# Longer runs in a transposed load, single buffers for small stores, and a new division of side work around a selective scan

## The chip, the cores and the metric

The kernel runs on one core of a Trainium2 chip. The metric is the device time of one execution in microseconds. A core has a matrix engine (TensorE, PE in the profile), VectorE (DVE), ScalarE (ACT), GpSimd (POOL) and SyncE (SP, which here issues all DMAs but the gathers), each with an instruction queue of its own that is worked off in order. 16 DMA engines serve the core.

## The reference, cut to what matters

Four layers over a tensor of 4 images, 128 channels and 128 x 128 pixels, each of the form x = x + f(group_norm(x)): a deformable 3x3 convolution (layer 0), a dilated convolution factored into three matrices (layer 1), a block around a two-dimensional selective scan (layer 2), and a 3x3 convolution that also takes differences of the channel sum (layer 3). The change concerns layer 2:

```python
x_flat = x.reshape(Bb, C, L)
x_t = x.transpose(0, 1, 3, 2).reshape(Bb, C, L)
x_hwwh = jnp.stack([x_flat, x_t], axis=1)
xs = jnp.concatenate([x_hwwh, jnp.flip(x_hwwh, axis=-1)], 1)
...
def step(h, inp):
    u, d, b, c = inp
    dA = jnp.exp(d[..., None] * A)
    h = h * dA + (d * u)[..., None] * b[:, :, None, :]
    y = jnp.einsum('bkcn,bkn->bkc', h, c)
    return (h, y)
...
return out_y[:, 0] + inv_y[:, 0] + wh_y + invwh_y
```

So the same image is scanned in four directions, two along rows and two along columns, with 16 states for each of 128 channels; the sums of the column directions come out in column order, and have to be read back in row order. Ahead of the scan lie a channel normalisation, projections and a depthwise convolution (layer2_pre); after it a normalisation, a gate, a projection and a second normalisation (layer2_post).

## The kernel before, in words

**Tiles.** An image is a matrix of 128 channels (partitions) by 16384 pixels, cut into 32 blocks of 512 pixels (four rows). Everything is float32. Between stages an image lives in DRAM.

**The scan.** `scan` (from L760) goes through 128 pairs of a direction and a block for each image, in the order of directions 0, 1, 3, 2. For each pair t it has four groups g of 32 channels, spread over 128 partitions as 32 channels x 4, and in each group four chunks: 16 chunks, each with one scan instruction on VectorE (L946) over 512 pixels. One such chunk is called a slot: 2048 slots an image, 8192 in all. For a group, a large VectorE product (L912) makes the inputs h from dub and bb; ScalarE makes the decays pa (L851, `decay`, into two PSUM buffers) and copies dub (L837, `inputs_up`); GpSimd multiplies the scanned h by cb (L885, `outputs`); TensorE sums over states (L862, `sums`) into yacc; `finish` copies yacc to y (L872) and stores it in yrow or ycol.

`prepare(t + 2)` (from L781) runs a piece at a time, one after each slot of t: a matmul pdt (L790), ScalarE's Abs into e (L795) and Relu into the first half of the tile steps (L798), more ScalarE work, a small matmul and its copy bc (L812), and four GpSimd instructions, the last of which (L822) writes the second half of steps. Steps and bc are then stored to DRAM (stepsd, bcd), and loaded back spread over the partitions (`spread_steps`, L830, two groups ahead; `spread_states`, L843).

At the start of an image nothing is running ahead, so two blocks are prepared at once:

```python
for t in range(2):
    for _ in prepare(t):
        pass
    fetch(t + 2)
flush()
```

**Stores.** `store` (L134) doesn't issue a DMA, it puts it on a list; `tick`, called once a slot, issues what is three ticks old, and `flush` issues all. All of it goes through SP's queue (L145, L149), as do all loads (L126), in the order of the program. An SP instruction that waits for its data or for a free buffer holds up those behind it.

**Side work.** While the scan of image b runs, the slots carry pieces of the other stages: layer2_post and layer3 of image b-1, then layer0_table, layer0, layer1 and layer2_pre of image b+1. `chain` gives each stage a weight; `together` advances the side work after each slot until its weighted progress has caught up with the scan's. A stage's weight thus decides over how many slots it is stretched. Weights: `head` (L1203) has layer0_table 12, layer0 28, layer1 14, layer2_pre 36; `tail` (L1206) has layer2_post 16, layer3 22; the rest of layer2_pre for image 0 has 18 (L1213). During the last scan the weights of `tail` are multiplied by 2.5, and layer2_post of the last image follows with 33 (L1217); it can take a block only once the last direction has summed it. The last image's layer3 runs alone at the end. Within a stage `weave` issues the steps of different blocks interleaved in a fixed order.

**Column sums.** In `layer2_post` (from L961), `fetch` (L987) loads for every CH = 16 image rows one tile ycols of 128 x 128 x 16 values from ycol (L992): its innermost run is 16 values, 64 bytes, at a distance of 512 bytes. `centre` multiplies four rows of it with a matrix (L1014), reading every 16th value. The transposed store of ucol in `layer2_pre` (cols, L744) works with CH = 32.

Of the kernel before, what the change touches and what calls it, by code (L numbers as in the profile page):

```python
# [10 lines left out]
F32 = mybir.dt.float32  # L11
# [99 lines left out]
def conv_preact_kernel(ctx: ExitStack, tc: tile.TileContext, a: dict, nb: int):  # L111
# [5 lines left out]
    dram = ctx.enter_context(tc.tile_pool(name="dram", bufs=2, space=DRAM))  # L117
    hp = ctx.enter_context(tc.tile_pool(name="sch", bufs=4))
    bp = ctx.enter_context(tc.tile_pool(name="scb", bufs=2))
    sp = ctx.enter_context(tc.tile_pool(name="scp", bufs=2))  # L120
    pss = ctx.enter_context(tc.tile_pool(name="scps", bufs=1, space=PSUM))
    psb = ctx.enter_context(tc.tile_pool(name="bgps", bufs=1, space=PSUM))

    def load(pool, src, shape, name, **kw):
        t = pool.tile(shape, F32, name=name, **kw)
        nc.sync.dma_start(t, src)  # L126
        return t
# [49 lines left out]

    xdt = load(const, a["xdt"], [DTR, NDIR, P], "xdt_sb")
    dtt = load(const, a["dtt"], [DTR, NDIR, P], "dtt_sb")
    wd = const.tile([P, NDIR, P], F32, name="wd")  # L180
    for k in range(NDIR):
        pw = bank(0, "pwd")
        nc.tensor.matmul(pw[:, 0:P], xdt[:, k, :], dtt[:, k, :], start=True, stop=True)
        nc.scalar.copy(wd[:, k, :], pw[:, 0:P])
    neg_a = load(const, a["alog"], [P, NDIR, NST], "neg_a")
# [5 lines left out]
    def blk(t, i):  # L191
        return t[:, i * N : (i + 1) * N]
# [567 lines left out]
    def scan(st, pull):  # L760
# [20 lines left out]
        def prepare(t):  # L781
# [13 lines left out]
            nc.scalar.activation(e, pdt, AF.Abs, bias=dtb)  # L795
            steps = sp.tile([P, 2, N], F32, name="steps")
            delta, du = steps[:, 0, :], steps[:, 1, :]
# [12 lines left out]
            nc.scalar.activation(one_e, one_e, AF.Identity, bias=minus)  # L810
            bc = sp.tile([2 * NST, N], F32, name="bc")
            nc.scalar.copy(bc, px[0 : 2 * NST])  # L812
# [56 lines left out]
        def finish(t):  # L869
            k, i, back, second = seq[t]  # L870
            y = sp.tile([P, N], F32, name="y")
            nc.scalar.copy(y, blocks[t]["y"])  # L872
            store(blk(ys[k % 2], i), y, of=ys)
            blocks[t] = None
            st["summed"] = t + 1 - 3 * NBLK
# [13 lines left out]
        for t in range(2):  # L889
            for _ in prepare(t):  # L890
                pass
            fetch(t + 2)
        flush()
# [7 lines left out]
        for t, (k, i, back, second) in enumerate(seq):  # L901
# [5 lines left out]
            for g in range(NG):  # L907
# [17 lines left out]
                if g == 3 and second:  # L925
                    c["before"] = load(sp, blk(ys[k % 2], i), [P, N], "before")
                for ng in range(NG):
# [33 lines left out]
    def layer2_post(st):  # L961
        CH = 16
        keep, stats_out = image("x3d"), new_stats(st["b"], 3)
        yrow, ycol = st["y"]
        urow = st["u"][0]
        with ExitStack() as s:
# [34 lines left out]
            def fetch_gate(i):  # L1001
                got["z", i] = load(lp, blk(st["z"], i), [P, N], "zl", bufs=5)
                got["y", i] = load(lp, blk(st["y1"], i), [HALF, N], "yl", bufs=5)

            def fetch_skip(i):
                got["x", i] = load(lp, blk(st["x2"], i), [P, N], "xl", bufs=4)

# [195 lines left out]
    def head(b):  # L1203
        return [(layer0_table(sts[b]), 12), (layer0(sts[b]), 28), (layer1(sts[b]), 14), (layer2_pre(sts[b]), 36)]

    def tail(b):  # L1206
        return [(layer2_post(sts[b]), 16), (layer3(sts[b]), 22)]

# [3 lines left out]
    for b in range(nb):  # L1212
        side = [(begun, 18)] if b == 0 else tail(b - 1)  # L1213
        if b < last:
            side += head(b + 1)
        else:
            side = [(stage, 2.5 * w) for stage, w in side] + [(layer2_post(sts[b]), 33)]  # L1217
        together(lambda pull: scan(sts[b], pull), chain(side))
# [85 lines left out]
```

## Time and profile before

| What | Time |
|---|---|
| Median of 3 runs | 23136.59 us (23130.67 to 23153.46) |
| The profiled execution itself | 23137.48 us |
| Its span, first to last instruction | 23135.7 us |
| VectorE busy | 18414.2 us (80%) |
| TensorE busy | 17549.8 us (76%) |
| GpSimd busy | 17326.7 us (75%) |
| ScalarE busy | 16509.2 us (71%) |
| DMA queue of SP, share of 16 engines' time | 50.2% |
| First scan instruction / last scan instruction | 2116.0 / 22807.9 us |

A line of the page's costliest groups names the line, the engine, the operation, what it writes and reads and its shape, how often it ran, then its busy time, the mean of one in ns, and the engine's idle time ahead of it with what ended most of that. TensorE works through a float32 matmul in two passes, so the records of matmuls are twice the number of matmuls in the code. TensorE's busy time is modelled and overlaps.

### The profile page before, as it was taken

What the parts mean: (1) busy time and instruction counts of PE and PEld (TensorE: products, weight loads), DVE (VectorE), ACT (ScalarE), POOL (GpSimd) and SP (SyncE); (2) the same over time, 40 slices, a digit from 0 to 9 for tenths busy, and PEclk for the clock granted to TensorE, in tenths of its full rate; (3) what the DMA queues carried; (4) which work ended last, traced back from release to release, by engine and by line L of the source; (5) the groups of instructions that cost most, each with busy time, mean ns of one, the idle gap of its engine ahead of it and who ended that gap; (6) DMA issues with size and microseconds to landing.
All of it is one profiled execution on the core that took longest, in us unless ns stands there. A gap on an engine that the chain in (4) does not pass through costs nothing. (4 is left out here: it accounts for less than half of the span.)

```text
span 23135.7 us, 180009 instructions
## 1 busy us (share of the span) xinstructions
PE 17549.8 (76%) x39144; PEld 6857.8 (30%) x39144; DVE 18414.2 (80%) x19279; ACT 16509.2 (71%) x37410; POOL 17326.7 (75%) x11422
## 2 busy tenths in 40 slices
PE   4558866667899897666789889666688978777778
PEld 1222322223333333222333334222233323233223
DVE  3553888888988799777897789877788789999973
ACT  5885768887677666788768676688877767666563
POOL 4762678888777877788876687788877678877773
PEclk7669987778999998777899999778799989899999
DMA  8775687777665958677766675877775667555664
GB/s 242 229 220 157 198 278 228 229 229 233 220 200 196 230 201 275 222 226 233 236 221 200 197 226 208 276 226 231 230 250 197 199 197 219 185 193 200 196 199 121
DMA packets 2557777, 5005.38 MB, mean 216 GB/s; under 512 B 1056832, under 2 KB 1328648, under 8 KB 2414352
## 3 DMA queue, kind: packets, MB, share of 16 engines
q1 hardware_dynamic: 2188048, 3785.60, 50.2%
q0 software_dynamic: 368640, 1208.25, 17.5%
q8 instruction: 317, 5.19, 0.1%
q14 instruction: 772, 6.32, 0.1%
HBM read 4065.12 MB, written 857.74 MB: 213 GB/s over the span
## 5 line engine op out<-in xcount | busy, mean ns | idle before, releaser
L885 POOL TENSOR_TENSOR h<-h,cb 128x1024 f32<-128x1024 f32 x4096 | 9620.6, 2357 | 3407.5 <-ACT carry L884 3261.6
L946 DVE TENSOR_TENSOR_SCAN h<-pa,carry,h 128x512 f32<-128x512 f32 x8192 | 10068.6, 1269 | 1601.4 <-ACT pa L851 1392.1
L862 PE MATMUL yacc<-h,gather_sb 128*128 128x512 f32 x16384 | 8716.5, 667 | 1293.3 <-POOL h L885 888.7
L851 ACT ACTIVATE pa<-spread,neg_a 128x512 f32<-128x512 f32 x8192 | 5616.0, 686 | 3173.9 <-DVE h L946 3143.2
L415 POOL DMA_INDIRECT g<-table,idx x4608 | 4391.2, 953 | 1543.8 <-issue 1116.2
L862 PEld LDWEIGHTS yacc<-h,gather_sb 128*128 128x128 f32 x16384 | 3331.8, 214 | 5889.4 <-issue 3897.2
L912 DVE TENSOR_TENSOR h<-dub,bb 128x2048 f32<-128x2048 f32 x2048 | 4641.1, 2266 | 430.6 <-ACT dub L837 421.7
L429 ACT ACTIVATE g<-g,wt 128x128 f32<-128x128 f32 x9216 | 2960.2, 391 | 1025.5 <-DMA g<-table,idx 1020.4
L452 PE MATMUL pst<-ident,v 128*128 128x128 f32 x4608 | 1193.7, 371 | 2475.2 <-DVE v L444 2232.2
L441 DVE TENSOR_TENSOR pw<-pw,g 128x512 f32<-128x512 f32 x2304 | 1604.3, 696 | 1641.9 <-ACT pw L429 1555.1
L452 PEld LDWEIGHTS pst<-ident,v 128*128 128x128 f32 x4608 | 727.5, 160 | 3892.8 <-issue 1628.1
L429 ACT ACTIVATE pw<-g,wt 128x128 f32<-128x128 f32 x4608 | 1690.9, 367 | 196.2 <-DVE v L444 84.2
L462 PE MATMUL acc<-smp,w_sb 128*128 128x512 f32 x2304 | 1610.2, 789 | 14.3 <-DVE x L469 11.3
L444 DVE SCALAR_TENSOR_TENSOR v<-g,wt,pw 128x128 f32<-128x128 f32 x4608 | 1292.8, 342 | 114.4 <-DVE pw L441 4.1
L837 ACT COPY dub<-spread 128x512 f32<-128x512 f32 x2048 | 1169.0, 571 | 131.0 <-DMA spread<-stepsd 131.0
L790 PE MATMUL pdt<-u,wd 128*128 128x512 f32 x1024 | 658.0, 729 | 795.2 <-DVE h L912 687.9
L884 ACT COPY carry<-h 128x2 f32<-128x2 f32 x4096 | 766.7, 187 | 677.9 <-DVE h L946 676.9
L806 PE MATMUL pxbc<-u,xbc_sb 128*128 128x512 f32 x1024 | 657.8, 728 | 655.0 <-DVE h L912 642.1
L1146 PE MATMUL p<-xn,w_l_sb 128*128 128x508 f32 (+2 forms) x2304 | 1102.0, 598 | 1.8 <-ACT xn L1125 1.8
L702 PE MATMUL px<-win,convw_sb 128*128 128x508 f32 (+1 forms) x1536 | 841.9, 630 | 6.8 <-DMA win<-win 6.8
L704 PE MATMUL py<-win,diag 128*64 128x508 f32 (+1 forms) x1536 | 836.1, 626 | 0.0
L816 POOL TENSOR_TENSOR e<-e,one_e 128x512 f32<-128x512 f32 x512 | 652.4, 1274 | 90.8 <-ACT one_e L810 90.8
(167 smaller groups left out, 16127.7 us busy)
## 6 DMA issues: line engine op xcount, KB each, us to landing
spread<-stepsd SPq DMA_DIRECT2D x2048, 512.0 KB
bb<-bcd SPq DMA_DIRECT2D x512, 1024.0 KB
cb<-bcd SPq DMA_DIRECT2D x512, 1024.0 KB
stepsd<-steps SPq DMA_DIRECT2D x512, 512.0 KB
table<-gt SPq DMA_DIRECT2D x512, 256.0 KB
g<-table,idx POOLq DMA_INDIRECT x4608, 3.8
u<-urow SPq DMA_DIRECT2D x256, 256.0 KB
yrow<-y SPq DMA_DIRECT2D x256, 256.0 KB
```

The costliest lines, as they stand in the source:

```text
L415: nc.gpsimd.indirect_dma_start(out=g[:, r].rearrange("p q c -> p (q c)"), out_offset=None, in_=table, in_offset=bass.IndirectOffsetOnAxis( ...
L429: nc.scalar.activation(pw[:, r * P : (r + 1) * P] if c == 0 else g[:, r, c, :], g[:, r, c, :], AF.Copy, scale=wv[:, r, q, k, c : c + 1],)
L441: nc.vector.tensor_add(pw, pw, g[:, :, c, :])
L444: nc.vector.scalar_tensor_tensor(v[:, r, :], g[:, r, 3, :], wv[:, r, q, k, 3:4], pw[:, r, :], ALU.mult, ALU.add)
L452: nc.tensor.transpose(pst[:, r * P : (r + 1) * P], v[:, r, :], ident)
L462: nc.tensor.matmul(got["a", i], w0[:, k, :], got.pop(("c", n)), start=k == 0, stop=k == KK - 1)
L837: nc.scalar.copy(p, blocks[t]["p", g][:, 1, :])
L851: nc.scalar.activation(pa, blocks[t]["p", g][:, 0, :], AF.Exp, scale=neg_a[:, k, n : n + 1])
L862: nc.tensor.matmul(c["y"], gather[:, g, :], c["h", g][:, ng, :], start=g == 0 and ng == 0, stop=last and not second,)
L885: nc.gpsimd.tensor_mul(h[:, sl, :], h[:, sl, :], cb[:, sl, :])
L912: nc.vector.tensor_tensor(h, c["pdu", g].unsqueeze(1).to_broadcast([P, NG, N]), c["bb"], ALU.mult)
L946: nc.vector.tensor_tensor_scan(o, f, o, carry[:, n : n + 1], ALU.mult, ALU.add)
```

## The change

Five things are done.

- Column sums are loaded for CH = 32 image rows at a time: tiles of 2 MB instead of 1 MB, with innermost runs of 128 bytes, half as many.
- Room for them: steps, bc, y and before get one buffer instead of two; zl and yl four instead of five; xl three instead of four.
- At the start of an image, `flush` is called after each prepared block, since with one buffer the first block's steps must be issued for storing before the second's are written.
- xdt and dtt, used once at the start, are put into a pool that is given back; the scan's pools are opened after that.
- Weights: layer0_table 11, layer0 27, layer1 13, layer2_pre 33, layer2_post 20, layer3 24; during the last scan those of `tail` are multiplied by 2.2.

```diff
@@ -175,13 +172,17 @@
-    xdt = load(const, a["xdt"], [DTR, NDIR, P], "xdt_sb")
-    dtt = load(const, a["dtt"], [DTR, NDIR, P], "dtt_sb")
     wd = const.tile([P, NDIR, P], F32, name="wd")
...
+    with tc.tile_pool(name="steps", bufs=1) as wp:
+        xdt = load(wp, a["xdt"], [DTR, NDIR, P], "xdt_sb")
+        dtt = load(wp, a["dtt"], [DTR, NDIR, P], "dtt_sb")
...
+    hp = ctx.enter_context(tc.tile_pool(name="sch", bufs=4))
+    bp = ctx.enter_context(tc.tile_pool(name="scb", bufs=2))
+    sp = ctx.enter_context(tc.tile_pool(name="scp", bufs=2))
@@ -793,7 +794,7 @@
-            steps = sp.tile([P, 2, N], F32, name="steps")
+            steps = sp.tile([P, 2, N], F32, name="steps", bufs=1)
@@ -808,7 +809,7 @@
-            bc = sp.tile([2 * NST, N], F32, name="bc")
+            bc = sp.tile([2 * NST, N], F32, name="bc", bufs=1)
@@ -868,7 +869,7 @@
-            y = sp.tile([P, N], F32, name="y")
+            y = sp.tile([P, N], F32, name="y", bufs=1)
@@ -889,6 +890,7 @@
         for t in range(2):
             for _ in prepare(t):
                 pass
+            flush()
             fetch(t + 2)
         flush()
@@ -923,7 +925,7 @@
-                    c["before"] = load(sp, blk(ys[k % 2], i), [P, N], "before")
+                    c["before"] = load(sp, blk(ys[k % 2], i), [P, N], "before", bufs=1)
@@ -959,7 +961,7 @@
     def layer2_post(st):
-        CH = 16
+        CH = 32
@@ -999,11 +1001,11 @@
-                got["z", i] = load(lp, blk(st["z"], i), [P, N], "zl", bufs=5)
-                got["y", i] = load(lp, blk(st["y1"], i), [HALF, N], "yl", bufs=5)
+                got["z", i] = load(lp, blk(st["z"], i), [P, N], "zl", bufs=4)
+                got["y", i] = load(lp, blk(st["y1"], i), [HALF, N], "yl", bufs=4)
...
-                got["x", i] = load(lp, blk(st["x2"], i), [P, N], "xl", bufs=4)
+                got["x", i] = load(lp, blk(st["x2"], i), [P, N], "xl", bufs=3)
@@ -1201,10 +1203,10 @@
-        return [(layer0_table(sts[b]), 12), (layer0(sts[b]), 28), (layer1(sts[b]), 14), (layer2_pre(sts[b]), 36)]
+        return [(layer0_table(sts[b]), 11), (layer0(sts[b]), 27), (layer1(sts[b]), 13), (layer2_pre(sts[b]), 33)]
...
-        return [(layer2_post(sts[b]), 16), (layer3(sts[b]), 22)]
+        return [(layer2_post(sts[b]), 20), (layer3(sts[b]), 24)]
@@ -1214,7 +1216,7 @@
-            side = [(stage, 2.5 * w) for stage, w in side] + [(layer2_post(sts[b]), 33)]
+            side = [(stage, 2.2 * w) for stage, w in side] + [(layer2_post(sts[b]), 33)]
```

More of the change, by code (lines that the diff above doesn't have):

```diff
@@ L117, in conv_preact_kernel @@
     dram = ctx.enter_context(tc.tile_pool(name="dram", bufs=2, space=DRAM))
-    hp = ctx.enter_context(tc.tile_pool(name="sch", bufs=4))
-    bp = ctx.enter_context(tc.tile_pool(name="scb", bufs=2))
-    sp = ctx.enter_context(tc.tile_pool(name="scp", bufs=2))
     pss = ctx.enter_context(tc.tile_pool(name="scps", bufs=1, space=PSUM))
@@ L175, in conv_preact_kernel @@
     nc.vector.memset(zero, 0.0)
-    xdt = load(const, a["xdt"], [DTR, NDIR, P], "xdt_sb")
-    dtt = load(const, a["dtt"], [DTR, NDIR, P], "dtt_sb")
     wd = const.tile([P, NDIR, P], F32, name="wd")
[L181 to L184, printed above, removed]
+    with tc.tile_pool(name="steps", bufs=1) as wp:
+        xdt = load(wp, a["xdt"], [DTR, NDIR, P], "xdt_sb")
+        dtt = load(wp, a["dtt"], [DTR, NDIR, P], "dtt_sb")
+        for k in range(NDIR):
+            pw = bank(0, "pwd")
+            nc.tensor.matmul(pw[:, 0:P], xdt[:, k, :], dtt[:, k, :], start=True, stop=True)
+            nc.scalar.copy(wd[:, k, :], pw[:, 0:P])
+    hp = ctx.enter_context(tc.tile_pool(name="sch", bufs=4))
+    bp = ctx.enter_context(tc.tile_pool(name="scb", bufs=2))
+    sp = ctx.enter_context(tc.tile_pool(name="scp", bufs=2))
     neg_a = load(const, a["alog"], [P, NDIR, NST], "neg_a")
```

## The prediction

> **What bounds the kernel now.** First the page's costliest groups, to see what one unit of the scan costs each engine. One slot is one scan instruction (L946); there are 8192, 2048 for each of four batches, and side work is dealt out between them.
>
> ```profile
> L885 POOL TENSOR_TENSOR h<-h,cb 128x1024 f32<-128x1024 f32 x4096 | 9620.6, 2357 | 3407.5 <-ACT carry L884 3261.6
> L946 DVE TENSOR_TENSOR_SCAN h<-pa,carry,h 128x512 f32<-128x512 f32 x8192 | 10068.6, 1269 | 1601.4 <-ACT pa L851 1392.1
> L912 DVE TENSOR_TENSOR h<-dub,bb 128x2048 f32<-128x2048 f32 x2048 | 4641.1, 2266 | 430.6 <-ACT dub L837 421.7
> ```
>
> A slot costs VectorE 1.269 + 2.266/4 = 1.836 us, whatever runs beside it. Since all 2048 slots of a batch are paid anyway, I count for each side stage its **excess**: its time minus 1.836 per slot. I then cut the trace at the first slot of each stage (the program's order gives the slots) and asked for busy time in each stretch. The columns are: length, busy PE, PE weight load, DVE, ACT, POOL, clock, DMA share, GB/s. Lines 1 to 5 are batch 0 (end of layer2_pre, then table, layer0, layer1, layer2_pre of the next batch); 6 to 11 are batch 1 (layer2_post, layer3, table, layer0, layer1, layer2_pre; batch 2 repeats it within 1%, layer2_post 592.8); 12 to 14 are batch 3 (layer2_post, layer3, its own layer2_post).
>
> ```profile
> 2115.90:2879.30 763.40, 687.26 (x1430) 237.59 (x1430) 619.27 (x439) 601.43 (x1102) 541.89 (x284) 0.97 0.59 192
> 2879.30:3337.80 458.50, 311.25 (x712) 125.82 (x712) 417.37 (x324) 286.72 (x574) 330.77 (x168) 0.85 0.89 301
> 3337.80:5570.40 2232.60, 1444.78 (x3459) 585.02 (x3458) 1808.67 (x2712) 1819.01 (x4944) 1887.35 (x1549) 0.79 0.70 227
> 5570.40:6115.70 545.30, 466.79 (x1011) 191.22 (x1010) 511.11 (x413) 354.26 (x697) 389.06 (x197) 0.94 0.73 242
> 6115.70:7585.00 1469.30, 1258.59 (x2592) 446.79 (x2592) 1207.92 (x857) 1084.39 (x2026) 1053.58 (x550) 0.95 0.58 195
> 7585.00:8188.80 603.80, 538.64 (x1091) 206.43 (x1092) 479.01 (x366) 440.41 (x867) 536.29 (x320) 0.96 0.89 233
> 8188.80:8868.80 680.00, 631.13 (x1513) 277.32 (x1512) 651.06 (x484) 422.48 (x844) 526.80 (x267) 0.97 0.58 204
> 8868.80:9277.60 408.80, 286.01 (x638) 117.50 (x637) 355.42 (x275) 248.09 (x493) 281.44 (x144) 0.80 0.90 302
> 9277.60:11386.30 2108.70, 1327.27 (x3283) 540.50 (x3283) 1671.41 (x2612) 1731.51 (x4755) 1763.93 (x1487) 0.78 0.71 227
> 11386.30:11853.50 467.20, 416.24 (x925) 173.43 (x925) 441.13 (x366) 307.69 (x605) 334.28 (x171) 0.96 0.78 255
> 11853.50:13156.60 1303.10, 1139.53 (x2338) 401.33 (x2338) 1019.11 (x722) 971.30 (x1790) 892.89 (x468) 0.94 0.58 192
> 18717.20:19999.00 1281.80, 1010.51 (x1955) 385.61 (x1956) 1152.33 (x848) 864.38 (x1731) 1101.68 (x608) 0.91 0.70 209
> 19999.00:21642.30 1643.30, 1279.62 (x2753) 517.88 (x2752) 1570.21 (x1138) 995.12 (x2013) 1300.08 (x660) 0.95 0.55 194
> 21642.30:22809.20 1166.90, 899.08 (x1688) 340.27 (x1688) 946.30 (x684) 713.64 (x1416) 899.70 (x492) 0.90 0.67 195
> ```
>
> The slots in these stretches are 350, 225, 525, 266, 682; 257, 358, 190, 443, 225, 575; 641, 880, 527. To see: layer3 runs on the VectorE floor (680.0 - 358 x 1.836 = 23 excess; 28 with 880 slots). layer2_post with 257 slots has 132 excess and POOL at 89%; with 641 it has 105. layer0 has 1295.
>
> Then the column sums and the matmul that reads them.
>
> ```profile
> L1014 PE MATMUL pd<-ycols,cmat_sb x256: 1017/1033/1043, 7610.5 to 22834.3; 128*128 128x512 f32 x128
> L992 SPq DMA_DIRECT2D ycols<-ycol x32: 547/594/685, 7575.6 to 22712.7; - x32
> ```
> ```profile
> L744 ACT COPY cols<-u x64: 1912/1957/2012, 1942.6 to 18661.9; 128x1024 f32<-128x1024 f32 x64
> ```
>
> Last, the start of a batch, in order of time (start, length).
>
> ```profile
> 7558.16 0.68 ACT L798 ACTIVATE steps<-pdt,vec_sb 128x512 f32<-128x512 f32 x1
> 7558.96 1.27 POOL L822 TENSOR_TENSOR steps<-steps,u 128x512 f32<-128x512 f32 x1
> 7568.69 0.79 SPq L149 DMA_DIRECT2D stepsd<-steps  x1
> 7571.83 2.59 SPq L830 DMA_DIRECT2D spread<-stepsd  x3
> 7578.30 16.32 SPq L126 DMA_DIRECT2D yrl<-yrow  x1
> ```
>
> The issue of yrl, just behind a ycols load, holds SP for 16.32 us.
>
> **What the skill says.** The Trainium skill, "DMA: Bandwidth & Descriptors", section on why small descriptors are slow: each packet carries a fixed cost beside its bytes. The trace agrees: by the semaphores, 1 MB of ycols in 64-byte runs lands a median of 17.6 us after issue, and 2 MB of ucol, stored in 128-byte runs, after 16.2; both have 16384 runs. The same page, on queues and rings: a ring is drained in order, so what is issued behind ycols waits; the 16.32 us above agrees. "SBUF — State Buffer", specifications: 16-byte lines, each crossing pays. L1014, stepping 64 bytes, takes 1033/512 = 2.02 ns an element where its neighbour L1012 takes 592/512 = 1.16; ScalarE stepping 128 bytes (L744) pays 1957/1024 = 1.91. So I take 128 bytes to cost what 64 do.
>
> **The change, part by part.** Compute instructions are unchanged in number; SP issues 16 fewer (9051 to 9035).
>
> *Shares.* The program's order after gives batches 1 and 2 layer2_post 320 slots, layer3 391, table 174, layer0 427, layer1 209, layer2_pre 527. Slopes of excess from the pairs above: table (45.4 - 60.0)/35 = -0.42 a slot, layer0 (1268.7 - 1295.4)/82 = -0.33, layer1 about 0, layer2_pre (217.1 - 247.4)/107 = -0.28. Donors therefore lose: table 16 x 0.42 = 7, taken as 9 since its DMA share is 0.90; layer0 16 x 0.33 = 5; layer2_pre 48 x 0.28 = 14; together +28. layer3 gains nothing. layer2_post: POOL's scan part is 526.8/358 = 1.47 a slot, so its own work is 536.3 - 257 x 1.47 = 158; with 320 slots POOL has 628. At today's 89% that is 706 us, at 93% (its share in the middle of the stage) 675; I take 690, fewer loads counted in. Excess 690 - 587.5 = 102, against 132: -30. Per batch -2; two batches -4.
> Batch 0: layer2_pre 370 first slots -6, table 218 +3, layer0 537 -4, layer2_pre 662 +6: -1. Batch 3: 54 slots pass from layer3 and the last stage to layer2_post (695, 833, 520); at 1.84 to 1.87 either way: 0. The last stage waits for the scan's blocks, so its share decides nothing.
>
> *Longer runs.* Eight ycols loads a batch become four, each about 17 us (bounds 16 to 20). VectorE's idle time around one in batch 3 exceeds that ahead of it by 2 us in the first stage and at most 5 in the last, where stretches with and without differ by 1.6. I take 2 and 1.5: 4 x 2 + 4 x 1.5 = -14. In batches 1 and 2 it is inside the 690. L1014 is taken at 0; the upper bound, twice its time, is 64 x 1.03 = 66 us of PE a stage.
>
> *Single buffers.* Relu into steps (L798) now waits until the last block's store has landed; behind it ScalarE queues dub and pa, and VectorE waits on those. For each block I compared landing and next Relu: the median slack is 8.8 us. Outside batch starts and two landings spoilt by a lost semaphore record, some 20 of 512 are late, 36 us together; pa is two deep, so half passes: +18 (0 to 36). bc has 16 us or more of slack, y 14, before 3: 0. At a batch start the second Relu ran at 7558.16; now it waits for du (7560.23) and its store (about 3 us): 5.2 later. SP has then already issued the first pair of stores, so the first spread goes about 3.5 us later, and nothing hides it: 4 x 3.5 = +14. (The added flush only orders those stores.)
> zl and yl with one buffer less would have waited in SP's queue on L1043 some 30 us per short stage, xl 12 on L1069; behind them stand spreads issued eight slots (about 18 us) early, which hides most: +6 (0 to 40).
> The hp, bp, sp pools opened later move addresses only: 0.
>
> **Sum** against the profiled execution (23137.5, span 23135.7): -1 - 4 - 14 + 18 + 14 + 6 = +19, so 23156; the median of the runs lies 1 us lower: 23155.
>
> **Rivals.** *Donors at their floors (slower).* In layer2_pre a returned slot saves only PE's scan share, (1258.6 - 1139.5)/107 = 1.11, so 48 slots cost 35 instead of 14; table by DMA 11, layer0 by ACT (1819.0 - 1731.5)/82 = 1.07, 12; layer1 10. That is 68 instead of 28, twice +40, and +9 in batch 0: 23244. For: PE 87 to 90% busy in layer2_pre, DMA 0.90 in table. Against: PE's time is modelled and overlaps, and the slopes above are measured. It decides from about 42 us a batch.
> *Strided read (slower).* L1014 doubles: 66 in each of two short posts where PE is at 89%: 23155 + 132 = 23287. Against: L744.
> *The blocked queue counted for more (faster).* Each removed load gives back 5 us: 8 x 5 = 40 in batch 3 instead of 14; layer2_post at 675 - 20 = 655 instead of 690, twice; stalls on steps 5 instead of 18: 23155 - 26 - 70 - 13 = 23046. For: ScalarE waited 32.6 us for x3d stores in the first short post, and longer steps would remove that. Against: POOL stays near its limit.
>
> **Numbers.** Measurement tells about 0.2% (46 us) from no change. Forecast 50% (own range 23100 to 23205), faster rival 22%, donors 20%, strided 8%. Of the forecast 6 points lie above 23183, of the faster rival 2 above 23091: faster 0.20, same 0.46, slower 0.34. The range reaches from the faster rival to a little past the donors.
>
> **What would show it.** ycols landing near 17 us with 16 loads; L1014 near 1033; short layer2_post near 690, layer2_pre near 1303.1 - 48 x 1.56 = 1228, table near 386; first h of a batch 3 to 4 us later. I am wrong if layer2_post in batch 1 comes below 660, or layer2_pre stays above 1245.

## The result, and the profile after

| | Before | Changed |
|---|---|---|
| Median of 15 runs each, same chip | 23139.98 us (23130.67 to 23153.46) | 23187.80 us (23179.60 to 23195.98) |
| Ratio, with its 95% interval | | 1.0021 [1.0013, 1.0029] |
| Span of the profiled execution | 23135.7 us | 23190.9 us |
| Granted TensorE clock, mean | 0.876 | 0.875 |

The change costs 47.8 us. The forecast was +19. Both lie in the forecast's range (23100 to 23205 us), but its sum hides errors that partly cancel, and these are what the runs below take apart.

First the page's costliest groups of the changed kernel, the lines that answer to those shown before (line, engine, operation, busy time, mean in ns, idle time ahead and its releaser).

```profile
L886 POOL TENSOR_TENSOR h<-h,cb 128x1024 f32<-128x1024 f32 x4096 | 9620.6, 2357 | 3449.2 <-ACT carry L885 3317.5
L948 DVE TENSOR_TENSOR_SCAN h<-pa,carry,h 128x512 f32<-128x512 f32 x8192 | 10070.5, 1270 | 1651.2 <-ACT pa L852 1441.8
L914 DVE TENSOR_TENSOR h<-dub,bb 128x2048 f32<-128x2048 f32 x2048 | 4646.7, 2269 | 427.4 <-ACT dub L838 416.5
```

A slot still costs VectorE 1.270 + 2.269/4 = 1.837 us. So the instructions of a slot ran no more slowly; VectorE's scan waited 50 us longer for pa (1441.8 against 1392.1). The place must be looked for stage by stage. The next view is the busy time by stretch (length, PE, PE weight load, DVE, ACT, POOL, clock, DMA share, GB/s), cut at the first slot of each stage. Lines 1 to 6 are batch 1: layer2_post, layer3, table, layer0, layer1, layer2_pre. Lines 7 to 9 are batch 3: layer2_post, layer3, its own layer2_post (line 9 ends at the start of the last scan, 1.3 us before the end that the table below uses).

```profile
7598.80:8288.80 690.00, 607.30 (x1229) 233.03 (x1229) 586.69 (x436) 512.68 (x1008) 628.28 (x368) 0.95 0.77 233
8288.80:9032.70 743.90, 671.51 (x1591) 291.10 (x1592) 710.94 (x534) 458.13 (x918) 575.25 (x292) 0.98 0.57 202
9032.70:9433.80 401.10, 252.78 (x603) 104.17 (x603) 330.34 (x260) 232.65 (x462) 259.19 (x132) 0.84 0.89 295
9433.80:11513.10 2079.30, 1290.20 (x3254) 532.47 (x3253) 1642.44 (x2585) 1708.35 (x4715) 1737.82 (x1474) 0.78 0.71 229
11513.10:11954.00 440.90, 395.92 (x887) 164.22 (x887) 413.58 (x348) 290.32 (x569) 310.68 (x159) 0.97 0.78 258
11954.00:13176.30 1222.30, 1080.89 (x2225) 377.64 (x2225) 935.87 (x662) 918.75 (x1682) 822.50 (x432) 0.94 0.58 191
18750.30:20138.90 1388.60, 1079.26 (x2077) 410.24 (x2078) 1246.93 (x915) 926.79 (x1858) 1181.77 (x649) 0.90 0.64 207
20138.90:21702.40 1563.50, 1231.46 (x2654) 501.02 (x2652) 1490.51 (x1081) 943.82 (x1908) 1231.64 (x625) 0.95 0.54 194
21702.40:22863.00 1160.60, 889.49 (x1664) 335.76 (x1664) 931.79 (x673) 702.89 (x1392) 886.35 (x487) 0.90 0.61 193
```

layer2_post of batch 1 takes 690.0 us with 320 slots, as forecast. The third line, the stage layer0_table, is the one to stop at: 401.1 us with 174 slots, where 386 was expected and 408.8 was measured with 190. Sixteen slots were taken from it and it gave back 7.7 us, 0.48 us a slot, where every slot costs VectorE 1.836.

As excess (time minus 1.836 per slot), for all batches; "alone" is the run e2 below, which changes the weights and nothing else:

| Stage (slots before, after) | Forecast | Before | After | Alone |
|---|---|---|---|---|
| Batch 0: layer2_pre, first (350, 370) | -6 | 120.7 | 120.5 | 120.6 |
| table (225, 218) | +3 | 45.5 | 45.1 | 45.6 |
| layer0 (525, 537) | -4 | 1268.7 | 1268.6 | 1272.1 |
| layer1 (266, 261) | 0 | 57.1 | 60.3 | 60.0 |
| layer2_pre (682, 662) | +6 | 217.2 | 227.7 | 227.8 |
| Batch 1: layer2_post (257, 320) | -30 | 131.8 | 102.4 | 100.4 |
| layer3 (358, 391) | 0 | 22.6 | 26.0 | 25.7 |
| table (190, 174) | +9 | 60.0 | 81.7 | 80.5 |
| layer0 (443, 427) | +5 | 1295.4 | 1295.4 | 1300.7 |
| layer1 (225, 209) | 0 | 54.2 | 57.1 | 56.1 |
| layer2_pre (575, 527) | +14 | 247.5 | 254.7 | 255.1 |
| Batch 2: layer2_post | -30 | 120.9 | 100.3 | 99.0 |
| layer3 | 0 | 21.7 | 24.2 | 25.5 |
| table | +9 | 59.9 | 79.0 | 80.6 |
| layer0 | +5 | 1299.6 | 1298.5 | 1301.8 |
| layer1 | 0 | 53.3 | 56.6 | 57.1 |
| layer2_pre | +14 | 245.1 | 255.3 | 254.8 |
| Batch 3: layer2_post (641, 695) | 0 | 104.8 | 112.5 | 117.2 |
| layer3 (880, 833) | 0 | 27.8 | 34.1 | 33.8 |
| its own layer2_post (527, 520) | 0 | 199.6 | 207.7 | 197.8 |

The forecast column holds the shares' part only. The differences between before and after sum to +54 us; the two profiled spans differ by 55. The column "alone" comes from another chip, so it is less exact: it sums to +59 against before, where the runs of e2 give +42.5. The kernel before itself has medians of 23140 to 23158 us on four of the five chips used here (23577 on the fifth), so sums over traces of different chips are uncertain by some 20 us.

In batches 1 and 2 the columns after and alone cut between layer2_post and layer3 one slot earlier than the column before does. Cut at the same place (321 and 390 slots), layer2_post has 107.7 and 103.8 (alone 105.2 and 103.6), and layer3 20.7 in both (alone 20.9). So layer2_post gains 24 and 17 us instead of 30, and layer3 loses nothing there.

Then the column sums, one view by tile, one of a line. After the counts stand least, median and most ns.

```profile
L1016 PE MATMUL pd<-ycols,cmat_sb x256: 1016/1028/1040, 7632.5 to 22889.3; 128*128 128x512 f32 x128
L994 SPq DMA_DIRECT2D ycols<-ycol x16: 547/594/648, 7590.7 to 22620.4; - x16
```
```profile
L745 ACT COPY cols<-u x64: 1916/1958/2012, 1940.5 to 18693.3; 128x1024 f32<-128x1024 f32 x64
```

The matmul that now steps 128 bytes takes 1028 ns, the one that stepped 64 took 1033: the distance makes no difference, as L745 (L744 before) had suggested. The loads are sixteen; by their semaphores they land a median of 20.3 us after issue (18.0 to 22.6), where the forecast took 17. The profile's page gives 20.9, which rests on one of them.

Last, the start of batch 1: selected lines in order of time, the changed kernel first, then the first h of before.

```profile
7573.62 0.32 SPq L146 DMA_DIRECT2D stepsd<-steps  x1
7576.56 0.69 ACT L799 ACTIVATE steps<-pdt,vec_sb 128x512 f32<-128x512 f32 x1 [4.92 <-DMA stepsd<-steps]
7585.22 0.32 SPq L146 DMA_DIRECT2D stepsd<-steps  x1
7587.58 1.94 SPq L831 DMA_DIRECT2D spread<-stepsd  x3
7591.92 18.84 SPq L123 DMA_DIRECT2D yrl<-yrow  x1
7596.45 2.29 DVE L914 TENSOR_TENSOR h<-dub,bb 128x2048 f32<-128x2048 f32 x1 [57.82 <-ACT dub L838]
```
```profile
7582.82 2.29 DVE L912 TENSOR_TENSOR h<-dub,bb 128x2048 f32<-128x2048 f32 x1 [57.22 <-ACT dub L837]
```

The brackets give the idle time of the engine ahead and what ended it. The Relu of the second block waits 4.92 us for the first block's store: the wait that the single buffer was to bring is there. VectorE's gap ahead of the first h, though, is 57.82 us and was 57.22 before.

### The profile page after: what moved, and what is told of

It reads as the page before. It is cut to its first block, busy times and chain, and to the rows that moved or that the text cites. A ratio compares the mean times of both kernels' runs of the same rounds, so it can differ in the third digit from the quotient of the medians.

```text
span 23190.9 us, 180836 instructions
## 1 busy us (share of the span) xinstructions
PE 17499.6 (75%) x39144; PEld 6843.8 (30%) x39144; DVE 18442.0 (80%) x19279; ACT 16512.0 (71%) x37410; POOL 17323.8 (75%) x11422
## 5 line engine op out<-in xcount | busy, mean ns | idle before, releaser
L948 DVE TENSOR_TENSOR_SCAN h<-pa,carry,h 128x512 f32<-128x512 f32 x8192 | 10070.5, 1270 | 1651.2 <-ACT pa L852 1441.8
```

Of the source, the lines that this page charges most:

```text
L948: nc.vector.tensor_tensor_scan(o, f, o, carry[:, n : n + 1], ALU.mult, ALU.add)
```

## Experiments

Three theories of the 48 us. **A**: the single buffer for steps is the larger part, in the scan and at the starts of batches. **B**: the weights are; the stages that gave up slots ran into other limits. **C**: a load of 2 MB stops SP's queue for longer than two of 1 MB do. Runs that were taken together share a chip and its runs of the kernel before; each "+" below is against the median of those.

**e1, the changed kernel with two buffers for steps.**

```diff
-            steps = sp.tile([P, 2, N], F32, name="steps", bufs=1)
+            steps = sp.tile([P, 2, N], F32, name="steps")
```

> The changed kernel with two buffers for steps again, all else as changed. Theory A (the single steps buffer is the larger part of the loss): ScalarE's waits of 78 us for the steps store go, the table stages fall from about 400 to about 384 us, and 30 to 50 of the 48 us come back: about 23148. Theory B (the stages that gave up slots ran into their floors): at most 10 come back: about 23178, table stages still near 398. Theory C (a load of 2 MB stops more than two of 1 MB): as B, with the losses around the loads of the last image unchanged.

Measured: 23186.88 against 23158.48, +28.4 us, ratio 1.0010 [1.0002, 1.0018]. A's wait is removed and most of the loss stays: 19.4 us come back, less than A expected (30 to 50) and more than B did (at most 10). The same place in its trace:

```profile
7575.96 0.68 ACT L799 ACTIVATE steps<-pdt,vec_sb 128x512 f32<-128x512 f32 x1
7587.04 1.90 SPq L831 DMA_DIRECT2D spread<-stepsd  x3
7595.86 2.29 DVE L914 TENSOR_TENSOR h<-dub,bb 128x2048 f32<-128x2048 f32 x1 [52.63 <-ACT dub L838]
```

The gap at the start is 52.63 us, below both 57.22 (before) and 57.82 (changed). So the added flush, which the forecast took to "only order those stores", saves 3.0 to 4.7 us at each of the four starts: the first block's store is out before the second's, and where both the flush and the single buffer are in (the changed kernel) the first spread is used 8.2 us after its issue instead of 10.4. The single buffer takes about the same amount away. Of the 19.4 us between e1 and the changed kernel, 17.8 lie at the four starts in the traces, and next to nothing in the scan.

**e2, the weights alone on the kernel before.**

```diff
-        return [(layer0_table(sts[b]), 12), (layer0(sts[b]), 28), (layer1(sts[b]), 14), (layer2_pre(sts[b]), 36)]
+        return [(layer0_table(sts[b]), 11), (layer0(sts[b]), 27), (layer1(sts[b]), 13), (layer2_pre(sts[b]), 33)]
...
-        return [(layer2_post(sts[b]), 16), (layer3(sts[b]), 22)]
+        return [(layer2_post(sts[b]), 20), (layer3(sts[b]), 24)]
...
-            side = [(stage, 2.5 * w) for stage, w in side] + [(layer2_post(sts[b]), 33)]
+            side = [(stage, 2.2 * w) for stage, w in side] + [(layer2_post(sts[b]), 33)]
```

> The kernel before with the new weights alone. Theory A: the gain in layer2_post and what its donors give up cancel within 15 us: 23125 to 23155. Theory B: 35 to 60 us slower than before, 23175 to 23200, with the loss in layer2_pre, table and layer1. Theory C: about as A.

Measured: 23200.94 against 23158.48, +42.5 us, 1.0019 [1.0012, 1.0025]: nearly the whole loss. B holds; its stages stand in the table above. To see why the stage layer0_table ("the table") gives so little back, I cut its stage at its first store into the table. Busy time by stretch, kernel before, from the first of these stores to the last blocks: batch 1 and batch 2 (144 slots each), then batch 0 (168 slots).

```profile
8961.00:9246.40 285.40, 208.46 (x457) 89.23 (x457) 255.33 (x184) 197.47 (x390) 212.07 (x109) 0.82 1.00 335
14520.80:14803.40 282.60, 205.52 (x457) 88.08 (x457) 255.14 (x185) 197.10 (x390) 212.20 (x109) 0.84 1.01 338
2990.10:3306.20 316.10, 225.44 (x507) 94.06 (x508) 295.96 (x212) 223.98 (x446) 245.28 (x126) 0.87 0.99 332
```

The same with the weights alone, 132 slots, batches 1 and 2; the last line is the whole stage in batch 1.

```profile
9123.60:9396.60 273.00, 183.47 (x429) 79.76 (x429) 234.93 (x170) 182.44 (x361) 193.78 (x99) 0.86 1.00 330
14700.60:14977.40 276.80, 188.23 (x429) 81.20 (x429) 235.25 (x170) 182.55 (x361) 193.80 (x99) 0.84 1.00 326
9038.40:9438.40 400.00, 252.53 (x605) 104.55 (x604) 330.56 (x260) 232.20 (x462) 259.38 (x132) 0.83 0.89 296
```

In this phase the DMA share is 1.00: DMA is taken to be the bound. (The share is no exact measure of full. The phase's first 50 us are below it, and the rest, in the kernel before, reads as the line below, with a share over 1. No run changed the bytes of this phase, so that DMA is the bound is read from the share and the rate.)

```profile
9005.00:9230.00 225.00, 164.07 (x369) 70.74 (x368) 199.31 (x143) 159.89 (x314) 167.13 (x85) 0.83 1.06 355
```

With 144 slots the engines move 335 GB/s x 285.4 us = 95.6 MB, with 132 slots 330 x 273.0 = 90.1 MB, so a slot brings (95.6 - 90.1)/12 = 0.46 MB in batch 1; in batch 2 it is (95.5 - 90.2)/12 = 0.44. The phase got shorter by 12.4 and 5.8 us, 0.76 us a slot on average, while each returned slot costs 1.836 where it goes. At an unchanged rate 0.45 MB a slot would have given back 1.3 us a slot; the rate fell as well, from 335 to 330 and from 338 to 326 GB/s.

The whole stage shows 0.89 only because it begins and ends with stretches of lower share (0.68 and 0.56 before). The last one, five slots in each kernel, got longer too (before, then the weights alone):

```profile
9246.40:9277.60 31.20, 16.28 (x88) 5.41 (x88) 9.01 (x8) 6.56 (x13) 4.47 (x3) 0.78 0.56 201
9396.60:9438.40 41.80, 18.53 (x90) 6.13 (x91) 11.46 (x13) 9.14 (x18) 5.34 (x3) 0.67 0.55 184
```

So of the 20.5 us by which batch 1's excess rises, 9.6 lie in the phase and 10.6 behind it; in batch 2 it is 16.2 of 20.7 and 4.3. That the part behind it is the same limit, queued transfers draining, is not shown.

The forecast's slope was drawn from batch 0 to batch 1, 225 to 190 slots, and used below 190, where it is steeper. With 168 slots the phase takes 316.1/168 = 1.88 us a slot, just above VectorE's 1.836, at a share that is already 0.99. For batch 1 alone e8, further down, gives 47.8 us of excess with 221 slots: 0.39 a slot from there to 190, and 20.5/16 = 1.28 from 190 to 174.

**e3, the single steps buffer and the flush alone.**

```diff
-            steps = sp.tile([P, 2, N], F32, name="steps")
+            steps = sp.tile([P, 2, N], F32, name="steps", bufs=1)
...
+            flush()
             fetch(t + 2)
```

> The kernel before with one buffer for steps and the added flush alone. Theory A: slower by 15 to 35 us (23155 to 23175), with waits of ScalarE for the steps store in the table stages and behind the ycols loads; less than in the changed kernel, since the table stages have more slots here. Theory B and C: within 10 us of before.

Measured: 23169.40 against 23158.48, +10.9 us, 1.0004 [0.9995, 1.0012]. Not to be told from no change, and less than A expected (15 to 35). Its gaps ahead of the first h are 57.45, 57.70 and 58.10 us in batches 1 to 3, with 57.22, 57.68 and 56.37 before.

**e4, the rest alone**: the changed kernel with the weights of before and two buffers for steps (so with flush, longer runs, and the other buffers).

```diff
-            steps = sp.tile([P, 2, N], F32, name="steps", bufs=1)
+            steps = sp.tile([P, 2, N], F32, name="steps")
...
-        return [(layer0_table(sts[b]), 11), (layer0(sts[b]), 27), (layer1(sts[b]), 13), (layer2_pre(sts[b]), 33)]
+        return [(layer0_table(sts[b]), 12), (layer0(sts[b]), 28), (layer1(sts[b]), 14), (layer2_pre(sts[b]), 36)]
...
-        return [(layer2_post(sts[b]), 20), (layer3(sts[b]), 24)]
+        return [(layer2_post(sts[b]), 16), (layer3(sts[b]), 22)]
...
-            side = [(stage, 2.2 * w) for stage, w in side] + [(layer2_post(sts[b]), 33)]
+            side = [(stage, 2.5 * w) for stage, w in side] + [(layer2_post(sts[b]), 33)]
```

> The kernel before with loads of ycols for 32 rows and the single buffers of bc, y, before, four of zl and yl, three of xl, the added flush and the moved pools, but two buffers for steps and the old weights. Theory A: within 15 us of before (23125 to 23155). Theory B: the same. Theory C: slower by 15 to 30 us (23155 to 23170), in the layer2_post stages, above all the two of the last image's scan.

Measured: 23152.13 against 23158.48, -6.4 us, 0.9996 [0.9988, 1.0004]. The gaps at the starts are 52.59, 53.07 and 52.93 us, so the flush should give some 19 us in all (4.6 in batches 1 and 2, 3.4 in batch 3 and 6.1 ahead of batch 0); the short layer2_posts lost part of it (excess 137.2 and 133.8, before 131.8 and 120.9). Longer runs brought no gain here, and C, which expected 15 to 30 us more, did not come either. The three parts sum to 42.5 + 10.9 - 6.4 = 47.0, near the 47.8 of the whole; it is not a clean division, since the flush is in two of them.

**e5, the weights alone with the table's back at 12, layer3's 23** (shown against e2).

```diff
-        return [(layer0_table(sts[b]), 11), (layer0(sts[b]), 27), (layer1(sts[b]), 13), (layer2_pre(sts[b]), 33)]
+        return [(layer0_table(sts[b]), 12), (layer0(sts[b]), 27), (layer1(sts[b]), 13), (layer2_pre(sts[b]), 33)]
...
-        return [(layer2_post(sts[b]), 20), (layer3(sts[b]), 24)]
+        return [(layer2_post(sts[b]), 20), (layer3(sts[b]), 23)]
```

> The kernel before with the new weights, but layer0_table back at 12 and layer3 at 23 instead of 24. Theory B, now with its place (the table's writing phase moves bytes as fast as the DMA engines can, about 50 MB of its own plus 0.32 MB for each slot at 335 GB/s, so slots taken from it give back half of their time): table stages fall from 400 to about 409 us with 190 slots again, that is from 80 to 60 us over the floor of 1.836 a slot, and 30 to 42 us of the 42 us loss of the weights alone come back: 0 to 12 us over before. If layer2_pre or layer0 were the place: at most 10 come back, 32 or more over before.

Measured: 23158.64 against 23145.39, +13.3 us, 1.0004 [0.9996, 1.0013]. The table's stretch in batch 1:

```profile
9003.70:9417.00 413.30, 277.73 (x640) 113.37 (x640) 357.96 (x280) 250.66 (x498) 282.63 (x144) 0.83 0.89 299
```

It has 190 slots again and an excess of 413.3 - 190 x 1.836 = 64.5 (63.4 in batch 2), where e2 has 80.5 and 80.6. That is 33 us of the trace, and the loss of the runs fell by 29; layer3 of batches 1 and 2, with 16 slots fewer, has the excess that it had (20.8, in e2 20.9). So the table's slots are the larger part of the loss. In this trace batches 1 and 2 are 13 and 4 us shorter than before, and what is left lies in batches 0 and 3, 15 us each.

**e6, the loads' whole cost**: the kernel before without seven of eight ycols loads of an image.

```diff
-                if got.get("from") != y:
+                if "from" not in got:
```

> The kernel before with the first ycols load of each layer2_post only; the other seven are left out, and the first tile is read in their place (the column sums of the other rows are not used). If the loads hold the scan up by 4 to 5 us each (the faster rival): 28 fewer give 110 to 140 us. If what they cost is mostly hidden (the forecast, 1.5 to 2 each in the last image and some in the short stages): 30 to 70 us faster than before. If they cost nothing: within 15 us.

Measured: 23090.90 against 23145.39, -54.5 us, 0.9974 [0.9965, 0.9983]. The stretches of batch 3 (layer2_post, then its own):

```profile
18705.50:19964.50 1259.00, 1006.68 (x1955) 384.36 (x1956) 1151.82 (x847) 863.65 (x1731) 1101.70 (x608) 0.91 0.60 207
21607.90:22773.30 1165.40, 895.40 (x1688) 338.09 (x1686) 944.70 (x682) 713.15 (x1415) 898.34 (x492) 0.91 0.55 189
```

Batch 3's layer2_post gives up 23 us (1281.8 before) for seven loads, 3.3 us each; the last stage gives up nothing (1166.7 us to the end of its last scan, 1166.6 before; the line above ends at the start of that scan). With almost all loads gone the whole gain is 54 us, so halving their number could not give the 110 that the faster rival counted for them.

**e7, the changed kernel with 16 rows a load again** (two tiles of 1 MB).

```diff
-        CH = 32
+        CH = 16
```

> The changed kernel with ycols in loads of 16 rows, as before; the single buffers and the new weights stay. If the longer runs gain what was forecast (14 us in the last image, more in the short stages): 15 to 30 us slower than the changed kernel, 63 to 80 over before. If the long runs bring nothing: within 12 us of the changed kernel, 36 to 60 over before.

Measured: 23196.36 against 23145.39, +51.0 us, 1.0022 [1.0015, 1.0030]; with 32 rows +47.8 [1.0013, 1.0029]. The longer runs, half as many, change nothing that can be measured. In the trace they cost the last stage 13 us (207.7 against 194.6 here). One part of it is seen behind the loads there. First SP's queue and ScalarE in the changed kernel, ahead of and at such a wait:

```profile
21759.78 18.16 SPq L123 DMA_DIRECT2D yrl<-yrow  x1
...
21778.52 0.38 SPq L142 DMA_DIRECT2D stepsd<-steps  x1
21778.94 0.52 SPq L831 DMA_DIRECT2D spread<-stepsd  x1
...
21783.13 0.69 ACT L799 ACTIVATE steps<-pdt,vec_sb 128x512 f32<-128x512 f32 x1 [4.88 <-DMA stepsd<-steps]
```

The issue behind a 2 MB load holds SP for 18.16 us, the store of steps stands behind it, and ScalarE waits 4.88 us for that. It does so behind all four loads of that stage (4.88, 2.62, 2.39, 3.01). In e1, with two buffers and the same loads, the stage has some 201 us of excess, so about half of the 13 goes with this wait. Over the whole program ScalarE waits for this store 78.0 us in 23 places. About 20 of these are the four starts, and 33 (17.1 and 16.0, six waits each) the tables of batches 1 and 2, where the excess is the same with two buffers (81.2 and 80.2 in e1): there DMA is taken to be the bound, and the wait costs nothing that shows.

**e8, other weights on the kernel before**, with what e2 and e5 had shown: more slots for the table, fewer for layer3, which runs on VectorE's floor.

```diff
-        return [(layer0_table(sts[b]), 12), (layer0(sts[b]), 28), (layer1(sts[b]), 14), (layer2_pre(sts[b]), 36)]
+        return [(layer0_table(sts[b]), 14), (layer0(sts[b]), 27), (layer1(sts[b]), 13.5), (layer2_pre(sts[b]), 35.5)]
...
-        return [(layer2_post(sts[b]), 16), (layer3(sts[b]), 22)]
+        return [(layer2_post(sts[b]), 19), (layer3(sts[b]), 19)]
```

> The kernel before with weights 14, 27, 13.5, 35.5 for layer0_table, layer0, layer1, layer2_pre and 19, 19 for layer2_post, layer3: slots taken from layer3, which loses nothing by it while it stays on VectorE's floor, given to the table (222) and to layer2_post (304). Theory B: table 60 to 46 us over the floor, layer2_post 127 to 103, layer3 near 25: 50 to 75 us faster than before. If layer3 meets a floor of its own at 300 slots (TensorE): layer3 rises to 40 to 60 over the floor and 0 to 35 are left. If the weights as such don't matter: within 15 us.

Measured: 23122.59 against 23145.39, -22.8 us, 0.9990 [0.9983, 0.9996]. Batch 1, layer2_post (305 slots), layer3 (311), table (221):

```profile
7593.20:8268.70 675.50, 591.92 (x1199) 227.22 (x1200) 562.74 (x426) 495.59 (x975) 606.70 (x356) 0.95 0.86 232
8268.70:8872.30 603.60, 575.03 (x1411) 259.50 (x1410) 570.52 (x425) 371.80 (x738) 460.10 (x234) 0.98 0.57 205
8872.30:9325.90 453.60, 306.11 (x707) 123.76 (x706) 411.10 (x317) 283.23 (x566) 325.70 (x165) 0.86 0.87 293
```

The table's excess falls to 453.6 - 221 x 1.836 = 47.8. layer3's rises to 32.6, so it is at its floor no longer, and the gain is the smaller one that was expected for that case (0 to 35), though layer3 rose less than expected then (40 to 60).

**e9, the loads split**: the kernel before with each ycols tile (16 rows) loaded by four DMAs of 32 columns, one a step of the stage.

```diff
+            def quarter(y, q):
+                w = slice(q * 32, (q + 1) * 32)
+                nc.sync.dma_start(
+                    got["c", y][:, w, :], ycol.rearrange("p (w h) -> p w h", h=H)[:, w, y : y + CH]
+                )
...
-                if got.get("from") != y:
-                    got["from"] = y
-                    got["c"] = lp.tile([P, W, CH], F32, name="ycols", bufs=2)
-                    nc.sync.dma_start(
-                        got["c"], ycol.rearrange("p (w h) -> p w h", h=H)[:, :, y : y + CH]
-                    )
+                s = NBLK - 1 - i
+                if s == 0:
+                    got["c", y] = lp.tile([P, W, CH], F32, name="ycols", bufs=2)
+                    for q in range(4):
+                        quarter(y, q)
+                elif s % 4 >= 2 and y >= CH:
+                    if s % 4 == 2:
+                        got["c", y - CH] = lp.tile([P, W, CH], F32, name="ycols", bufs=2)
+                    quarter(y - CH, s % 4 - 2)
+                elif s % 4 < 2 and s >= 4:
+                    quarter(y, s % 4 + 2)
+                got["c"] = got["c", y]
```

> The kernel before with each ycols load cut into four DMAs of 4096 runs of 64 bytes, issued one a step of layer2_post instead of all at once. All the loads together cost 35 to 55 us (the run without them). If what costs is that one load fills the queues and holds SP's next DMA for some 15 us: no issue of more than 5 us behind them, and 20 to 40 us faster than before. If what costs is the engines' time for the runs themselves: within 10 us of before.

Measured: 23520.29 against 23576.63, -56.3 us, 0.9975 [0.9964, 0.9985]. That is more than was expected (20 to 40), and as much as leaving the loads out (e6), though as many bytes and as many runs move. But how much of it is the split is not clear: on the chip of e9 and e10 the part ahead of the first scan took 2538 us in e9's trace and 2561 in e10's instead of 2116, though the code there is the same, and there is no trace of the kernel before on that chip. From the first scan on, e9's trace is 29 us shorter than that of before on its own chip. The following runs put the split at 20 to 30 us, too.

**e10, e8 and e9 together**: the weights of e8 and the loads of e9.

> The rebalanced weights (14, 27, 13.5, 35.5, 19, 19) and the loads in four parts together. If both gains are of different places they add: 23 us from the weights and 20 to 40 from the parts, 43 to 63 us faster than before. If the short layer2_post is bound by GpSimd whatever the loads do: 23 to 35 us.

Measured: 23519.02 against 23576.63, -57.6 us, 0.9978 [0.9969, 0.9987]. By the runs this is not better than e9. The traces tell why: from the first scan on e10's is 27 us shorter than e9's, about what e8's weights gained (22.8), and the 23 us that it took longer ahead of the first scan hide that.

**e11, the changed kernel with its loads split**: four DMAs of 32 columns and 32 rows, on four steps of eight. Only what differs from e9's edit is shown.

```diff
...
+                elif 2 <= s % 8 < 6 and y >= CH:
+                    if s % 8 == 2:
+                        got["c", y - CH] = lp.tile([P, W, CH], F32, name="ycols", bufs=2)
+                    quarter(y - CH, s % 8 - 2)
...
```

> The changed kernel with each ycols load of 32 rows cut into four DMAs of 4096 runs of 128 bytes, issued in four successive steps of layer2_post. If the changed kernel got nothing from its longer runs because each load still comes as 16384 runs in one piece: 25 to 50 us faster than the changed kernel, about as fast as before (within 20 us), with layer2_post below 680 us in the short stages and below 1375 in the long one. If the hold comes from the bytes or from the single buffers: within 12 us of the changed kernel.

Measured: 23185.29 against 23158.01, +27.3 us, 1.0012 [1.0006, 1.0019]; unsplit it was +47.8. The gain of some 20 us is short of what was expected (25 to 50, and within 20 of before). SP's queue around one load, in order of time, first the changed kernel, then this one:

```profile
19021.59 0.64 SPq L994 DMA_DIRECT2D ycols<-ycol  x1
19022.32 14.91 SPq L123 DMA_DIRECT2D yrl<-yrow  x1
19037.32 0.38 SPq L123 DMA_DIRECT2D url<-urow  x1
```
```profile
19084.89 0.59 SPq L991 DMA_DIRECT2D ycols<-ycol  x1
19085.53 4.58 SPq L123 DMA_DIRECT2D yrl<-yrow  x1
19090.16 0.43 SPq L123 DMA_DIRECT2D url<-urow  x1
```

One hold, the time that the issue behind a load takes, falls from 14.91 to 4.58 us. Over the program it stands so:

| Kernel | Loads | Median hold | Longest | Sum |
|---|---|---|---|---|
| before | 32 | 15.3 us | 17.2 us | 478 us |
| changed | 16 | 18.3 | 19.4 | 282 |
| e11 | 64 | 6.4 | 9.2 | 388 |
| e9 | 128 | 6.2 | 9.4 | 750 |

Within each pair of equal weights and run length (before and e9, changed and e11) the split kernel holds SP for longer in sum and is faster, by some 20 us in the second pair, where the two intervals still overlap, and by 29 to 56 in the first: the sum of the holds is not what counts. That it is the length of a single one fits spreads issued eight slots ahead (8 x 1.836 = 14.7 us on VectorE's floor, some 17 at the pace of the changed layer2_post): a hold of 6 us is covered, one of 18 is not. A load in four parts also fills the DMA engines for a shorter time at once, and no run separates the two.

**e12, the kernel of e10 again**, on a chip where the part ahead of the first scan takes 2122 us.

> The rebalanced weights and the loads in four parts, once more beside the kernel before, since in the earlier comparison the part ahead of the first scan differed by 23 us between the two new kernels. If the gains add: 45 to 75 us faster than before. If not: 20 to 40.

Measured: 23105.99 against 23158.01, -52.0 us, 0.9978 [0.9969, 0.9986]; its span is 23098.2 us. That is what was expected if the gains add (45 to 75): with e8's 22.8 taken off, 29 are left for the split. It is faster than both kernels.

## Why the prediction was right and where it was wrong

The time fell into the range; slower by more than 0.2% had been given 0.34, no change 0.46, and the measured 0.21% stands at that border. The stated sum of +19 was too low by 29 us. That it was no further off is in part luck. The shares were forecast at -5 and cost 42 us in the runs of e2 alone; the longer runs were forecast at -14 and brought nothing; against that, the buffers were forecast at +38 and, with the flush, cost next to nothing (e3 and e4, which hold them all, sum to +4.5).

- **"layer2_post: ... I take 690"**: right, 690.0 and 687.8. The way to it (POOL's own work of 158 us plus 1.47 a slot, at 91% busy) carries. The fewer loads that were counted in had no part in it: e2, with loads of 16 rows, has as little excess.
- **Table, "16 x 0.42 = 7, taken as 9"**: failed: about +20 in each of two batches, so a miss of 22 us. The slope came from two points above a bend and was used below it, and the mean DMA share of 0.90 for the stage was read as room, where its writing phase stood at 1.00. e5 shows it: with the 16 slots back, 29 of the 42 us go. The slower rival named this very limit ("table by DMA 11") and had half its size.
- **layer2_pre +14, layer0 +5, layer1 0**: +8 and +10, 0 (+5 and +2 with the weights alone), +2 to +4. The first was too high, and the rival's 35, 12 and 10 were far too high: layer2_pre gave back (1303.1 - 1222.3)/48 = 1.68 us a slot, so PE's 87% was not a limit there. All donors together lost 35 and 36 us a batch with the weights alone; forecast 28, rival 68, and its point of decision was 42. So the rival did not come true as stated. It was right on the place in the table only.
- **"Batch 0 ... -1. Batch 3 ... at 1.84 to 1.87 either way: 0"**: failed, and the largest miss of all. Alone, the weights cost about +17 in batch 0 (10.6 of it in the next image's layer2_pre; the first part of layer2_pre did not gain its 6) and +17 in batch 3. In batch 3 of the changed kernel 54 slots more cost layer2_post (1388.6 - 1281.7)/54 = 1.98 us each, and 47 fewer gave layer3 back (1643.3 - 1563.5)/47 = 1.70. Small differences from the floor count when so many slots move. Where they come from is not shown.
- **Longer runs, -14**: failed; e7 puts them at 0 within its interval. The step that failed is pricing by the number of loads: a load twice as large lands after 20.3 instead of 17.6 us and holds SP for 18.3 instead of 15.3, and in batch 3's layer2_post four of them cost as much as eight small ones (excess 112.5, in e7 113.6). The Trainium skill, "DMA: Bandwidth & Descriptors", section on why small descriptors are slow, puts a fixed cost on each packet; with 16384 runs in either load, that the landing grew by only 16% while the bytes doubled agrees. That the queue would be held for longer behind each load was left out of the price.
- **Relu into steps, mid-scan +18**: failed. The waits exist (some 58 us of ScalarE beside the starts), but more than half of them stand in the table, where DMA is taken to set the pace. In the scan e1 and the changed kernel differ by about 2 us in the traces.
- **Batch start, "nothing hides it: 4 x 3.5 = +14", "the added flush only orders those stores"**: failed. The single buffer does cost about 5 us a start (e1), but the flush saves about as much. In batch 1, counted from the first block's Relu, the first spread is issued 22.6 us later instead of 20.3, and it is used after 8.2 us instead of 10.4; against before the first h comes 0.6, 0.0 and 1.5 us later.
- **zl, yl, xl +6; L1016 0**: in the first short layer2_post SP waits 20 us for zl and yl and 12 for xl (forecast 30 and 12), in waits of 1.4 us on average; what came of them was not measured by itself. The matmul is as forecast, and the strided rival is refuted.
- **The faster rival**: refuted by e6 and e7.

So A fell as the larger part (19 of 48 us, nearly all at the starts), B held with its main place in the table, and C is not shown: e4 and e7 find no loss by the larger loads, and only the last stage of the trace has one.

What stays open: why layer1 loses 3 us a batch and layer3 of batch 3 loses 6; what the 15 to 17 us in each of batches 0 and 3 come from; and how much of e9's 56 us is the split, since its chip took 2538 to 2561 us for the same code ahead of the first scan.

## What to carry to other kernels

Before taking slots from a stage, cut it into phases and look for one in which a shared resource stands at 1.00: its mean over the stage hides that, and a slope across the bend overstates what it gives back. For a large transfer in a shared in-order queue, compare its longest single hold with the lead of what is queued behind it; here neither the number of loads nor the sum of the holds told the cost. Splitting the loads over steps brought some 20 to 30 us, leaving them out 54. Where a buffer is taken away and an order is changed in one edit, price the two apart: here each was worth some 3 to 5 us a start, with opposite signs.

## What was not expected of the hardware

- With 16384 runs in one DMA, runs of 64 bytes land after a median of 17.6 us and runs of 128 bytes after 20.3: twice the bytes for 16% more time.
- In the table's writing phase the DMA share was 1.00 at 335 GB/s, and 1.06 at 355 in its full part. The Trainium skill, "Perfetto Trace Analysis", section "Roofline", gives about 435 GB/s as the sum of a core's 16 engines and sets it as the ceiling where a core runs alone; with this mix of transfers the share stood at full well below that. The section also gives 358 GB/s as a core's share of the HBM when both cores of a pair use it. Only one core ran here, but 355 lies close to that figure, and no run tells whether the engines or the memory behind them set the limit.
- The same page, section "DMA Optimizations", advises larger transfers, and splitting where the engines are mostly idle. In this kernel only the second held: larger +0 (e7), split some 20 us (e11) to 56 us, 0.9975 [0.9964, 0.9985] (e9).
